# Seven products of two-by-two parts in place of eight, for the queries and values of a graph attention layer

## The chip, the core and the metric

The kernel runs on one core of a Trainium2 chip. The metric is the device time of one execution in microseconds (us), as the median of several runs. The engines named below are TensorE (PE in the profile; PEld are its weight loads), VectorE (DVE), ScalarE (ACT), and SyncE (SP), which issues the transfers. Each engine takes its instructions from a queue of its own, in order, and waits there until what an instruction needs is ready.

## The reference

Four graph layers stand one after the other, each as `x = x + layer(relu(layernorm(x)))`, on `x` of 128 graphs x 64 nodes x 256 features in float32. The first is a graph convolution, the second a spectral one (eigenvectors), the third a graph network with LSTMs over windows of nodes, and the fourth, where the change lies, an attention over the 512 edges of the graph with 4 heads of 64:

```python
Xq = (H @ W_lin.T).reshape(bt, n, h, dh)
Xv = (H @ W_val.T).reshape(bt, n, h, dh)
Qs, Kt = Xq[:, src], Xq[:, dst]
e = einsum('behd,hd->beh', leaky_relu(Qs + Kt, 0.2), a) + log(A0[src, dst] + eps)
attn = softmax of e over the edges of one source
Y = segment_sum(attn[..., None] * Xv[:, dst], src)
return Y @ W_out.T
```

The change concerns the first two lines: the queries `Xq` and the values `Xv`, two products of the same 8192 x 256 matrix with 256 x 256 weights.

## The kernel before

All matrices are float32. In the fourth layer (`layer3`) the 8192 rows are cut into 16 blocks of 512 rows (`BT`), a block into 4 tiles of 128 rows (`TPB`). Half a block, 256 rows or 4 graphs, is a group `g`; eight groups share one softmax (`q = g // 8`). Steps of the loop over `g`:

- `turned` normalizes a block (ACT writes `h`, one instruction a tile, from statistics `n_st`, `n_mv`, `n_r`, `n_m` of DVE) and transposes it on PE (`ps<-ident,h`) into `hT`: two chunks of 128 features, each 128 x 512. DVE copies the first chunk out of PSUM, ACT the second (`move` takes the two in turn).
- `queries` multiplies each of the 4 tiles with `WQV` (`w3_qv`, 256 x 512: columns 0 to 255 are `W_lin`, 256 to 511 are `W_val`) in two accumulating matmuls of 512 columns, one for each chunk. ACT copies the left half to `Q`, DVE the right half to `V` (tile `XV`). Then DVE multiplies `Q` with the vector `a` (`lin_p`) and sums it up by heads (`lin`).
- `score` is 8 matmuls (`ps<-ed_S,Q`), each followed by a ReLU on ACT (`r`). `reduce` is 8 matmuls of `r` into the bank `acc` (`acc<-r,ed_apad`). `softmax` works on DVE and ACT on a whole `acc` (tiles `sm_e`, `sm_m`), and `edgewise` transposes its result into `at`.
- `between` builds the attention matrices: DVE forms four products `aw` of 1024 columns for a group, PE sums them (`ps<-aw,ed_ODT`), ACT copies the sum to `an`. There are 5 buffers of `aw`, so DVE waits for PE to release one. `weighted` is 16 small matmuls of `an` with `V`, whose result DVE and ACT copy to `y` in halves. `output` is 4 matmuls (`ps<-w_o,y`) and an addition on DVE into `X`, which is then stored.
- `back`, in the first eight groups, transposes the third layer's result (`ls_t`) for a block and adds it to `X`.

`turned` and `queries` run one block ahead of `score`, in the odd groups. `between`, `weighted` and `output` run 10 groups behind it (`LAG`), so that blocks 6 and later have all the steps, and the earlier ones only a part. The pool `l3ps` has 5 PSUM banks for all tiles `ps`.

The order in which the steps are written is not quite the order in the queues: a scheduler in the framework sets, when the kernel is built, the order of each engine's instructions by its own estimate of durations, and the chip keeps to it. For an ordinary block the queue of PE before the change is: transposes, `output`, the eight matmuls of `queries`, `score`, `weighted`, `reduce`, `between`, then for the second half `output`, `score`, `weighted`, `reduce`, `between`.

Every operation is recorded under the line of a helper (L799), so groups are told apart by the names of their tiles.

Of the kernel before, what the change touches and what calls it, by code (L numbers as in the profile page):

```python
# [8 lines left out]
F32 = mybir.dt.float32  # L9
I32 = mybir.dt.int32  # L10
AF = mybir.ActivationFunctionType
# [64 lines left out]
class Eig:  # L76
# [12 lines left out]
    def t(self, name, *shape, dt=F32):  # L89
        key = (name, shape)  # L90
        if key not in self.tiles:
            n = "e_" + name + "_" + "_".join(map(str, shape))
            self.tiles[key] = self.pool.tile([64, *shape], dt, name=n)
        return self.tiles[key]
# [748 lines left out]
class Plan:  # L843
# [56 lines left out]
    def rest(self):  # L900

        while any(self.queue.values()):
            for e in self.queue:
                self.fill(e, 1e9)
# [8 lines left out]
class Fast:  # L913
# [229 lines left out]
    def scale(self):  # L1143
# [32 lines left out]

        Q = t("Q", 64, 2, 64)
        o.ts(Q[:, 0, :], D[:], mid[:], ALU.subtract, sc[:], ALU.mult)
        nes = self.NE = t("NEs", 64, 64)
        o.ts(nes[:], NE[:], sc[:], ALU.mult)  # L1180
        o.stt(Q[:, 1, :], nes[:], -1.0, nes[:], ALU.mult, ALU.mult)
        self.ne2 = Q[:, 1, :]
        p = self.mm((self.k.ones[0:1, :], Q[0:1, :, :].rearrange("p a b -> p (a b)")), p=128, n=128)
        DD, E2 = self.DD, self.E2 = t("DD", 128, 64), self.ME[:, 1, :]
# [258 lines left out]
B, N, D = 128, 64, 256  # L1443
P = 128
NB = 16
TPB = 4
BT = 512
# [18 lines left out]
class Kernel:  # L1466
# [949 lines left out]
    def layer3(self):  # L2416
        nc, o, io = self.nc, self.o, self.io
        cx, (w,) = self.stage([("l3x", 1)], "tile")
        with cx:
            cy, pools = self.stage([("l3", 2), ("l3v", 2), ("l3s", 1), ("l3r", 6), ("l3ps", 5), ("l3cps", 1), ("l3yps", 1)], "tile")  # L2420
            with cy:
                self.a02 = self.everywhere(w, "ed_a", io["L3_gnn_a"].rearrange("h d -> (h d)"))
                o.ts(self.a02[:], self.a02[:], 0.2, ALU.mult)
                self.drop, self.dropr = (w.tile([P, E], F32, name="ed_" + n) for n in ("drop", "dropr"))
                o.ts(self.drop[:], self.cont[:], 1.0, ALU.subtract, FLOOR, ALU.mult)
                o.ts(self.dropr[:], self.contr[:], 1.0, ALU.subtract, FLOOR, ALU.mult)
                WQV = w.tile([P, 2, 2 * D], F32, name="w3_qv")
                for x, n in enumerate(("W_lin", "W_val")):
                    nc.sync.dma_start(WQV[:, :, x * D:(x + 1) * D],
                                      io[f"L3_gnn_{n}_t"].rearrange("(k p) m -> p k m", p=P))  # L2430
                WO = self.weights(w, "w3_o", io["L3_gnn_W_out_t"])


                st, LAG = {}, 10
                self.turned(st, 0, *pools)
                self.queries(st, 0, WQV, *pools)
                for g in range(8 * NG + LAG + 2):
                    v, busy = g - LAG, g < 8 * NG
                    ahead = (g + 1) // 2 if g % 2 and g + 1 < 8 * NG else None
                    if busy:  # L2440
                        self.score(st, g, *pools)
                    if busy and v >= 1:
                        self.weighted(st, v - 1, *pools)
                    if busy:
                        self.reduce(st, g, *pools)
                    if g % 8 == 1 and 1 < g < 8 * NG + 2:
                        self.edgewise(st, g // 8 - 1, *pools)
                    if 0 <= v < 8 * NG:
                        self.between(st, v, *pools)
                    if not busy and v <= 8 * NG:  # L2450
                        self.weighted(st, v - 1, *pools)
                    if busy and g % 8 == 7:
                        self.softmax(st, g // 8, *pools)
                    if ahead:
                        self.turned(st, ahead, *pools)
                    if g < 8:
                        self.back(8 + g, pools[4], "ps")
                    if busy and v >= 1:
                        self.output(st, v - 1, WO, *pools)
                    if not busy and g > 8 * NG:  # L2460
                        self.output(st, v - 2, WO, *pools)
                    if ahead:
                        self.queries(st, ahead, WQV, *pools)

    def turned(self, st, i, pool, vp, sp, rp, psum, psc, psy):

# [2 lines left out]
        for dc in range(2):  # L2469
# [2 lines left out]
                self.nc.tensor.transpose(p[:, j * P:(j + 1) * P], h[:, j, dc * P:(dc + 1) * P], self.ident[:])  # L2472
            self.move(hT[:, dc, :], p[:])

    def queries(self, st, i, WQV, pool, vp, sp, rp, psum, psc, psy):

        o, hT = self.o, st["hT"]
        Q = rp.tile([P, TPB, D], F32, name="Q", bufs=2)
        V = st["V", i] = rp.tile([P, TPB, D], F32, name="XV", bufs=7)
        st["Q", i] = Q  # L2480
        for j in range(TPB):
            p = psum.tile([P, BT], F32, name="ps")
            for kc in range(2):
                self.mm(p[:], hT[:, kc, j * P:(j + 1) * P], WQV[:, kc, :], kc == 0, kc == 1)
            self.act(Q[:, j, :], p[:, 0:D], AF.Copy)
            o.copy(V[:, j, :], p[:, D:2 * D])

        if i % 4 == 0:
            st["lin", i // 4] = pool.tile([P, 2, 2, 8, HEADS], F32, name="lin")
            self.nc.vector.memset(st["lin", i // 4][:], 0.0)  # L2490
        lin, pr = st["lin", i // 4], sp.tile([P, TPB, D], F32, name="lin_p")
        o.mul(pr[:], Q[:], self.a02[:, None, :].to_broadcast([P, TPB, D]))
        k = 2 * (i % 4)
        for x in range(2):
            s = slice(64 * x, 64 * x + 64)
            o.red(lin[s, x, :, k:k + 2, :].rearrange("p m a h -> p a m h"),
                  pr[s].rearrange("p (a m) (h d) -> p a m h d", m=2, h=HEADS), ALU.add)
# [161 lines left out]
```

## Time and profile before

| | |
|---|---|
| median of 3 runs | 2345.04 us (2342.6 to 2351.49) |
| profiled execution | 2348.6 us, of it the span of the profile 2346.8 us |
| mean granted clock of TensorE | 0.993 |
| PE busy | 2293.6 us |
| DVE busy | 1602.6 us |
| ACT busy | 1134.3 us |
| fourth layer | from about 1750 us to the end |
| 1900 to 2250 us of the span | PE 349.38, DVE 201.44, ACT 138.67 of 350 us busy |

A line of a group gives line, engine, operation, output<-inputs, partitions x elements and the number of records, then the busy time in us, the mean of one in ns, and the idle time of the engine ahead of it with what ended it. A float32 matmul leaves two records, so that 256 records are 128 matmuls. A line of the timeline gives the start and the duration in us, the engine, and in brackets the idle time ahead of it and its releaser. A matmul's recorded end is modelled and reaches over the start of the next one, so the time that PE needs for a row of matmuls is read from start to start.

### The profile page before, as it was taken

The numbers are of one execution on the slowest core, as the hardware profiler recorded it, in microseconds if no ns is written. First come the engines' busy times: TensorE is split into PE (matmuls) and PEld (weight loads), VectorE is DVE, ScalarE is ACT, GpSimd is POOL, SyncE is SP. The second block draws the span as 40 slices with busy tenths as digits, with TensorE's granted clock in tenths as the row PEclk, the third lists the DMA queues.
The fourth block names the chain that finished last, engine by engine and source line by source line (L and its number), as shares of the span: only waits on it lengthen the run. The fifth ranks groups of instructions, "written<-read, shape, count | busy, mean of one in ns | idle before, by whom it ended". The sixth has DMA issues, their size and how long they took to land.

```text
span 2346.8 us, 32591 instructions
## 1 busy us (share of the span) xinstructions
PE 2293.6 (98%) x12153; PEld 1629.2 (69%) x12153; DVE 1602.6 (68%) x4006; ACT 1134.3 (48%) x2490; POOL 2.9 (0%) x26
## 2 busy tenths in 40 slices
PE   7999998999999999999999999999999999999989
PEld 4555446986777788888999998888874444444434
DVE  7877676998447777666777667569655566556467
ACT  5665864654436654444444434347445544344321
POOL 0000000000000000000000000000000000000000
PEclk9999999999999999999999999999999999999989
DMA  5000221230010000001000001000020000000001
GB/s 170 1 2 19 64 63 27 73 82 19 1 36 1 1 19 1 1 1 37 1 1 1 1 14 59 1 1 17 1 72 1 1 10 14 14 19 14 15 14 50
DMA packets 61192, 54.86 MB, mean 23 GB/s; under 512 B 15203, under 2 KB 58852, under 8 KB 61028
## 3 DMA queue, kind: packets, MB, share of 16 engines
q1 hardware_dynamic: 61028, 52.73, 7.3%
q8 instruction: 96, 1.57, 0.3%
q14 instruction: 68, 0.56, 0.1%
HBM read 35.93 MB, written 16.78 MB: 22 GB/s over the span
## 4 chain that ended last, share of the span: by engine, by line
PE 80%; DVE 3%; issue 0%; ACT 0%; ACTq 0%; DVEq 0%
PE ps L799 69%; PE acc L799 5%; PE pt L799 4%; PE pe L799 1%; DVE sm_m L799 1%; PE y L799 1%; DVE X L799 1%; DVE aw L799 0%; ACT ls_g L799 0%; DVE ls_g L799 0%; DVE sm_e L799 0%; DVE ls_t L799 0%; DVE XV L799 0%; DVE y L799 0%; DVE n_st L799 0%
## 5 line engine op out<-in xcount | busy, mean ns | idle before, releaser
L799 ACT ACTIVATE ls_g<-ls_g,ls_b 128x512 f32<-128x512 f32 (+4 forms) x472 | 242.9, 565 | 153.2 <-DVE ls_g L799 151.4
L799 ACT ACTIVATE ls_g<-ps,ls_b 128x256 f32<-128x256 f32 (+3 forms) x268 | 115.3, 470 | 330.6 <-PE ps L799 327.3
L799 PE MATMUL ps<-z,w 128*128 128x512 f32 x512 | 259.1, 630 | 0.9 <-ACT z L799 0.9
L799 PE MATMUL ps<-big,X 128*128 128x176 f32 (+3 forms) x848 | 212.9, 366 | 0.8 <-ACT big L799 0.7
L799 DVE TENSOR_TENSOR aw<-at,ed_OST 128x1024 f32<-128x1024 f32 x128 | 150.0, 1220 | 92.7 <-PE ps L799 92.7
L799 DVE TENSOR_TENSOR ls_g<-ls_z,ps 128x512 f32<-128x512 f32 (+5 forms) x256 | 146.9, 579 | 91.4 <-PE ps L799 90.0
L799 PE MATMUL ps<-ls_tx,X 128*128 128x160 f32 (+2 forms) x960 | 207.0, 326 | 0.6 <-ACT ls_g L799 0.6
L799 PE MATMUL ps<-X,X 128*128 128x160 f32 (+1 forms) x896 | 199.1, 306 | 0.0
L799 PE MATMUL ps<-X,ls_w 128*128 128x256 f32 x640 | 190.5, 379 | 0.0
L799 PEld LDWEIGHTS ps<-ls_tx,X 128*128 128x128 f32 x960 | 161.8, 190 | 15.4 <-DVE X L799 5.2
L799 PEld LDWEIGHTS ps<-big,X 128*128 128x128 f32 x848 | 145.9, 190 | 30.6 <-issue 19.4
L799 DVE TENSOR_TENSOR X<-ls_g 128x1024 f32<-128x1024 f32 (+2 forms) x108 | 117.4, 1087 | 51.1 <-ACT ls_g L799 51.1
L799 ACT ACTIVATE r<-ps 128x512 f32<-128x512 f32 x256 | 129.3, 625 | 41.4 <-PE ps L799 41.3
L799 PEld LDWEIGHTS ps<-X,X 128*128 128x128 f32 x896 | 148.4, 190 | 0.0
L799 PE MATMUL ps<-X,ls_s 128*128 128x256 f32 x480 | 142.3, 379 | 0.0
L799 PEld LDWEIGHTS ps<-z,w 128*128 128x128 f32 x512 | 88.8, 193 | 71.1 <-issue 62.6
L799 PE MATMUL ps<-ls_tx,ls_s 128*128 128x256 f32 x464 | 134.7, 379 | 0.0
L799 PE MATMUL ps<-ls_tx,ls_w 128*128 128x256 f32 x464 | 133.3, 380 | 0.0
L799 PEld LDWEIGHTS ps<-X,ls_w 128*128 128x128 f32 x640 | 121.4, 190 | 16.8 <-DVE X L799 0.3
L799 PE MATMUL ps<-big,ls_w 128*128 128x256 f32 x464 | 131.9, 379 | 0.7 <-ACT ls_z L799 0.7
L799 PE MATMUL ps<-ed_S,Q 64*128 64x512 f32 x512 | 128.3, 617 | 0.9 <-DVE XV L799 0.9
L799 ACT ACTIVATE h<-X,n_m,n_r 128x256 f32<-128x256 f32 x192 | 99.6, 589 | 40.9 <-issue 25.0
(532 smaller groups left out, 4012.0 us busy)
## 6 DMA issues: line engine op xcount, KB each, us to landing
X<-in_x_dram SPq DMA_DIRECT2D x32, 512.0 KB
xs<-X SPq DMA_DIRECT2D x16, 512.0 KB
X<-xs SPq DMA_DIRECT2D x16, 512.0 KB
out_dram<-X SPq DMA_DIRECT2D x32, 256.0 KB
X<-in_L_gnn_Wih_t_dram SPq DMA_DIRECT2D x4, 512.0 KB
ls_w<-in_L_gnn_Wih_t_dram SPq DMA_DIRECT2D x4, 512.0 KB
ls_w<-in_L_gnn_Whh_t_dram SPq DMA_DIRECT2D x4, 512.0 KB
w<-in_L_gnn_W_t_dram SPq DMA_DIRECT2D x2, 512.0 KB
```

The costliest lines, as they stand in the source:

```text
L799: i = method(*a, **kw)
```

## The change

The queries and values of a block are seen as one product of two-by-two parts. `A[t][k]` is `hT`'s chunk `k` (128 features) of the 256 rows `t`; `B[k][x]` is chunk `k` of `W_lin` (`x = 0`) or `W_val` (`x = 1`). The 4 results, queries and values of the two halves of the rows, took 8 products of parts. They now take 7, by Strassen's scheme in Winograd's form; a product of parts is two matmuls of 256 columns, one for each tile of 128 rows, so that a block has 14 matmuls of 256 columns instead of 8 of 512.

`sums3` forms four sums of the weights once, on DVE. In a block DVE forms three sums of `hT` ahead of the products (S3, S1 in the place of `A[1][0]`, S2) and a fourth later; all are 128 x 256. Product 1 goes to PSUM bank a, 6 to b, 7 to f, 5 to d; ACT copies bank a to `Z` (half of `V`), and only then does product 2 add into bank a, which ACT copies to half of `Q`. DVE adds b to `Z`, forms `U` (the other half of `V`) from `Z` and f, and adds d to `U`; after that products 4 and 3 add into f and d, and two further additions on DVE give the other half of `Q` and finish `Z`. `queries` now returns its second part (`rest`: products 2, 4 and 3 and their results), which is called after `output`, the first part being called ahead of it. `Q` has one buffer instead of two. The work on `lin` is the same, in a function of its own.

In the built kernel the queue of PE for an ordinary block is now: transposes, `weighted`, products 1, 2, 6, 7, 5, `output`, products 4 and 3, `score`, `reduce`, `between`; its second half is as before. In blocks 9 and 13 six of the sixteen matmuls of `weighted` stand between products 1 and 2.

```diff
--- before.py
+++ after.py
@@ -2433,7 +2433,8 @@
 
                 st, LAG = {}, 10
                 self.turned(st, 0, *pools)
-                self.queries(st, 0, WQV, *pools)
+                WQV = self.sums3(w, WQV)
+                self.queries(st, 0, WQV, *pools)()
                 for g in range(8 * NG + LAG + 2):
                     v, busy = g - LAG, g < 8 * NG
                     ahead = (g + 1) // 2 if g % 2 and g + 1 < 8 * NG else None
@@ -2455,12 +2456,14 @@
                         self.turned(st, ahead, *pools)
                     if g < 8:
                         self.back(8 + g, pools[4], "ps")
+                    if ahead:
+                        rest = self.queries(st, ahead, WQV, *pools)
                     if busy and v >= 1:
                         self.output(st, v - 1, WO, *pools)
                     if not busy and g > 8 * NG:
                         self.output(st, v - 2, WO, *pools)
                     if ahead:
-                        self.queries(st, ahead, WQV, *pools)
+                        rest()
 
     def turned(self, st, i, pool, vp, sp, rp, psum, psc, psy):
 
@@ -2472,18 +2475,59 @@
                 self.nc.tensor.transpose(p[:, j * P:(j + 1) * P], h[:, j, dc * P:(dc + 1) * P], self.ident[:])
             self.move(hT[:, dc, :], p[:])
 
+    def sums3(self, w, WQV):
+
+        o = self.o
+        B = [[WQV[:, k, D * x:D * x + D] for x in range(2)] for k in range(2)]
+        T1, T2, T3 = (w.tile([P, D], F32, name=f"w3_t{n}")[:] for n in range(3))
+        o.sub(T1, B[1][1], B[0][1])
+        o.sub(B[0][1], B[0][1], B[0][0])
+        o.sub(T2, B[1][1], B[0][1])
+        o.sub(T3, B[1][0], T2)
+        return {1: B[0][0], 2: B[1][0], 3: B[1][1], 5: B[0][1], 7: T1, 6: T2, 4: T3}
+
     def queries(self, st, i, WQV, pool, vp, sp, rp, psum, psc, psy):
 
         o, hT = self.o, st["hT"]
-        Q = rp.tile([P, TPB, D], F32, name="Q", bufs=2)
+        A = [[hT[:, k, 256 * t:256 * t + 256] for k in range(2)] for t in range(2)]
+        S = sp.tile([P, 2, 256], F32, name="hS")
+        S1, S2, S3 = A[1][0], S[:, 0], S[:, 1]
+        o.sub(S3, A[0][0], A[1][0])
+        o.add(S1, A[1][0], A[1][1])
+        o.sub(S2, S1, A[0][0])
+        Q = st["Q", i] = rp.tile([P, TPB, D], F32, name="Q", bufs=1)
         V = st["V", i] = rp.tile([P, TPB, D], F32, name="XV", bufs=7)
-        st["Q", i] = Q
-        for j in range(TPB):
-            p = psum.tile([P, BT], F32, name="ps")
-            for kc in range(2):
-                self.mm(p[:], hT[:, kc, j * P:(j + 1) * P], WQV[:, kc, :], kc == 0, kc == 1)
-            self.act(Q[:, j, :], p[:, 0:D], AF.Copy)
-            o.copy(V[:, j, :], p[:, D:2 * D])
+        banks = {}
+
+        def product(a, m, bank, first):
+            if first:
+                banks[bank] = psum.tile([P, 2, D], F32, name="ps")
+            for u in range(2):
+                self.nc.tensor.matmul(banks[bank][:, u, :], a[:, u * P:(u + 1) * P], WQV[m], start=first and u == 0,
+                                      stop=u == 1, skip_group_check=True)
+            return banks[bank][:]
+
+        Z, U = V[:, 0:2, :], V[:, 2:4, :]
+        a = product(A[0][0], 1, "a", True)
+        self.act_copy(Z, a)
+        o.add(Z, Z, product(S2, 6, "b", True))
+        o.add(U, Z, product(S3, 7, "f", True))
+
+        o.sub(S3, A[0][1], S2)
+        o.add(U, U, product(S1, 5, "d", True))
+
+        def rest():
+            self.act_copy(Q[:, 0:2, :], product(A[0][1], 2, "a", False))
+            o.add(Q[:, 2:4, :], Z, product(A[1][1], 4, "f", False))
+            o.add(Z, Z, product(S3, 3, "d", False))
+            self.linear(st, i, pool, vp, sp, rp, psum, psc, psy)
+
+        return rest
+
+    def linear(self, st, i, pool, vp, sp, rp, psum, psc, psy):
+
+        o, Q = self.o, st["Q", i]
 
         if i % 4 == 0:
             st["lin", i // 4] = pool.tile([P, 2, 2, 8, HEADS], F32, name="lin")
```

## The prediction

> **What bounds the kernel now.** I read the page's busy shares first, then the waits of TensorE (PE) in the fourth layer, then the groups by form for durations, then the timeline of one block. Last I read the order of the instructions in the engines' queues, before and after the change, which is fixed when a kernel is built.
>
> Page, parts 1 and 2; after it all waits of PE between 1900 and 2250 us (us in total, times, longest):
> ```profile
> PE 2293.6 (98%) x12153; PEld 1629.2 (69%) x12153; DVE 1602.6 (68%) x4006; ACT 1134.3 (48%) x2490; POOL 2.9 (0%) x26
> PE   7999998999999999999999999999999999999989
> PE ps L799 <- DVE XV L799: 0.6, 1, 0.6
> ```
> PE never rests in this layer: 0.6 us in 350. So PE time saved is saved in full, and every new wait of PE is paid in full.
>
> Groups (busy us, mean ns of one); then two rows from the timeline of the third layer's Strassen products:
> ```profile
> L799 PE MATMUL ps<-w_qv,hT 128*128 128x512 f32 x256 | 112.7, 593 | 0.7 <-DVE hT L799 0.7
> L799 DVE TENSOR_TENSOR ls_tx<-big,ls_tx 128x256 f32<-128x256 f32 x96 | 40.3, 420 | 1.1
> L799 DVE TENSOR_TENSOR X<-X,ps 128x512 f32<-128x512 f32 x48 | 32.1, 681 | 19.4 <-PE ps L799 19.2
> 1500.21 0.59 PE L799 MATMUL ps<-ls_tx,ls_w 128*128 128x256 f32 x2
> 1500.64 0.59 PE L799 MATMUL ps<-X,ls_w 128*128 128x256 f32 x2
> ```
> A 256-column matmul comes every 0.43 us (1500.64 - 1500.21). An addition on VectorE (DVE) takes 0.42 for 256 columns, 0.68 for 512 out of PSUM.
>
> Timeline of one block (start, duration):
> ```profile
> 2049.22 3.50 DVE L799 TENSOR_TENSOR aw<-at,ed_OST 128x1024 f32<-128x1024 f32 x3 [4.84 <-PE ps L799]
> 2050.84 1.09 PE L799 MATMUL ps<-ident,h 128*128 128x128 f32 x8
> ...
> 2051.77 1.89 PE L799 MATMUL ps<-w_o,y 128*128 128x256 f32 x8
> 2051.97 0.60 ACT L799 ACTIVATE hT<-ps 128x512 f32<-128x512 f32 x1 [0.39 <-PE ps L799]
> 2052.46 2.06 ACT L799 ACTIVATE h<-X,n_m,n_r 128x256 f32<-128x256 f32 x4
> 2052.63 0.68 DVE L799 COPY hT<-ps 128x512 f32<-128x512 f32 x1
> ...
> 2053.50 7.03 PE L799 MATMUL ps<-w_qv,hT 128*128 128x512 f32 x16
> ...
> 2055.41 0.38 ACT L799 ACTIVATE Q<-ps 128x256 f32<-128x256 f32 x1 [0.89 <-PE ps L799]
> ...
> 2060.46 3.91 PE L799 MATMUL ps<-ed_S,Q 64*128 64x512 f32 x16
> ...
> 2064.92 3.65 PE L799 MATMUL acc<-r,ed_apad 128*64 128x512 f32 x16
> ```
> What the reader is to see: the transposes of `turned` end at 2051.77, but the DVE copy of hT ends only at 2053.31, since three `aw` products stand before it. The output projection (`w_o`, 1.73 us) fills exactly that hole.
>
> **What the change saves.** The 8 matmuls take 2060.46 - 2053.50 = 6.96 us; 14 of 0.43 take 6.03. That is 0.93 a block, and over 16 blocks 15 us. ScalarE (ACT) does two copies of 0.60 for four of 0.38, 0.3 less. DVE does four additions of 0.42 and five of 0.68 for four copies of 0.42: 3.4 more a block. It is busy 201 of 350 us here, so on average it has room; what counts is where these stand in its queue.
>
> **What the change costs: an ordinary block** (6, 7, 9 to 11, 13 to 15). PE's queue is now: transposes, the 16 small `weighted` matmuls (0.62, before behind the scores), product 1, 2, 6, 7, 5, `output`, 4, 3, scores. On the clock above:
> - The transposes and `weighted` end at 2052.39. Product 1 needs hT: 2053.31 + 0.05 = 2053.36. `output` no longer covers: 0.97 idle.
> - Product 1 ends at 2054.22. Product 2 adds into its bank, so ACT must first have copied it to V. In ACT's queue hT and four h stand before (to 2054.52), a half of y (0.40) and the copy (0.60, as for hT): 2055.52, product 2 at 2055.57. Idle 1.35. With ACT free it would still be 0.20 (from the end of two matmuls, 2055.21, to the Q copy at 2055.41) + 0.60 + 0.05 = 0.85.
> - Product 6 needs the sum S2. DVE after hT: y 0.42, S3 0.42, one `aw` 1.22, S1 0.42, a reciprocal 0.17, S2 0.42: 2056.38. Product 2 ends at 2056.43; no wait, with nothing to spare.
> - Products 6, 7, 5 end at 2059.02, `output` at 2060.75. DVE has read product 7's bank by about 2060.0 and product 5's by 2061.1, so products 4 and 3 run on, to 2062.47. Here `output` is the cover; without it 0.6 to 1.0 more.
> - Scores: the sixth needs the bank of product 3, which DVE reads only after the residual, Q and lin_p: 2065.1 against 2064.6. The eight take 3.98 instead of 3.84. `acc` starts at 2066.45, in the trace at 2064.92: **+1.5**.
>
> Eight such blocks: +12.
>
> **Blocks with a softmax, 8 and 12.** There the softmax is mixed with the new sums in DVE's queue. From the timeline of block 8:
> ```profile
> 1980.38 1.22 DVE L799 TENSOR_TENSOR_SCAN sm_m<-ed_drop,sm_e 128x512 f32<-128x512 f32 x1
> ...
> 1991.32 3.34 DVE L799 RECIPROCAL sm_m<-sm_m 128x512 f32<-128x512 f32 x1
> 1991.46 1.98 PE L799 MATMUL ps<-ed_S,Q 64*128 64x512 f32 x6 [0.62 <-DVE XV L799]
> ```
> Before S2 come two scans (2.2), S3, a maximum, S1 and a subtraction: S2 at 1985.2, product 2 ends at 1983.5, idle 1.7. Before product 5 is read come y, `aw`, two additions, two scans, a product and S3: 1992.4, where PE would be ready for product 3 at 1990.8. Before Q comes the reciprocal of 3.34: Q at 1997.8 frees the last score's bank. `acc` starts at about 1998.2 instead of 1995.05: +3.1 each, +6.
>
> **Early blocks**, by the same reckoning on their own timelines:
> - Blocks 1 to 3 have no `output` or `weighted` yet, and ACT's `ls_t` copy of 1.13 and two h stand before V's copy: product 2 idles 1.7, less 0.93, +0.7 each, +2.
> - Block 0: two DVE operations of 1.22 stand among the sums. hT ends at 1751.1, S2 at 1754.9, product 1 at 1752.7: idle 2.2, and 0.7 before product 4; less 0.93, +2.
> - Block 4 (softmax, no `aw`): hT ends at 1851.4; two scans, two residual additions, a maximum, a subtraction and the sums put S2 at 1857.7, product 2 ends at 1854.5: idle 3.2. Products 4 and 3 wait 1.1 and 1.0 behind scans and reciprocal. Less 0.93: +4.3.
> - Block 5: three `aw` among the sums put S2 at 1883.0, product 2 ends at 1881.2: 1.8. V's copy costs 1.1, the last score's bank 1. Less 0.93: +3.
>
> Together +11.
>
> **Beside the path.** The four weight sums are 1.7 us of DVE, once, in the third layer's end, where PE waits 1.5 us in 150: priced 0, between -1 (order changes) and +1.7. Q's single buffer: its last reader, the scores of the block before, ends some 10 us earlier: 0. Behind the last block nothing changes.
>
> Sum: 12 + 6 + 11 = **+29.6** unrounded. The profiled execution took 2348.6 (span 2346.8 and 1.8 around it), 3.6 above the median; it would become 2378. On the median: 2345 + 30 = **2375**. Bounds: only the 0.97 and the least copy wait of 0.85 in eight ordinary blocks (+0.9 each) and half of all the rest give +16; a third more on everything gives +39.
>
> **The clock.** Two idle times of PE near the end:
> ```profile
> 2270.71 0.69 PE L799 MATMUL y<-an,XV 64*64 64x64 f32 x32 [2.71 <-ACT y L799]
> ...
> 2279.68 1.12 PE L799 MATMUL ps<-ident,sm_e 128*128 128x128 f32 x4 [8.27 <-DVE sm_e L799]
> 2280.72 5.90 PE L799 MATMUL ps<-aw,ed_ODT 128*64 128x512 f32 x16
> ```
> Up to the end of 2.71 us idle the granted clock is 0.98 (2262 to 2272); during the 8.27 it falls to 0.50, and the two groups after it take 2.7 us longer than elsewhere (5.90 for 3.65, 1.12 for 0.66). My longest gap, 3.2 us, is nearest to the first: 0. Three such falls at the top of the range: +8.
>
> [...]
>
> **Rivals.**
> - The holes are covered, and PE keeps its saving: 2345 - 15 = 2330, faster. It decides between products 1 and 2 and before product 1: the two gaps must come to less than 0.93 a block. For it: in blocks 9 and 13 six `weighted` matmuls stand between products 1 and 2. Against it: in the others nothing does, and PE's queue is in order. 3%.
> - Only the copy of V shows, at its least (0.85), with DVE early enough everywhere: -0.93 + 0.85 = -0.1 a block, and up to +0.5 with ACT's queue: 2343 to 2353, no change. The `aw` that stand before hT in both kernels speak against it. 9%.
> - The gaps reach the length that halves the clock, in most of 16 blocks at 2.7: 2375 + 30 or more, 2405. Only the 8.27 us row speaks for it. 6%.
> - The products do not become shorter: the two rows at 0.43 exclude it, as weights and columns have the same shape.
>
> **Numbers.** The forecast has 82%. Range 2360 to 2393: from +16, to +39 with three falls of the clock (+47). A change of 0.5% (11.7 us) is about what a measurement of this kernel can tell from none. Faster 3%, same 9%, slower 88% (82 + 6).
>
> **What would show it.** Right: PE busy falls by about 15 us in the layer while its waits rise from 2.4 us (1750 to 2250) to some 45, most before product 1 (on hT), before product 2 (on XV by ACT), and in blocks 4, 5, 8 and 12 on hS or XV by DVE. Wrong: waits under 15 us in all; the wait on hT missing, as DVE's `aw` came earlier; a granted clock under 0.9 between 1750 and 2250.

## The result and the profile after

The changed kernel takes **2375.61 us** (median of four runs, 2373.75 to 2380.73) against 2348.2 of the kernel before on the same chip: the ratio is 1.0124, with a 95% interval of 1.0107 to 1.014. It is slower by 27.4 us, where 30 more than 2345 had been forecast.

The comparison of the two traces needs one caution. The span grew by 26.0 us only (2346.8 to 2372.8), because the first 400 us, which the change does not touch, ran 4 us shorter in this execution. So everything below goes by the length of the fourth layer alone, from the first transposes of block 0 to the end of the span: 597.1 us before, **627.5 after, +30.4**. A block's length is read from its transposes to those of the next. All these lengths are of one profiled execution of each kernel; where nothing differs, the blocks of two kernels agree within 0.01 us.

The page's busy shares, then TensorE's (PE's) waits from 1750 to 2250 us (us in total, times, longest):

```profile
PE 2292.5 (97%) x12345; PEld 1662.1 (70%) x12345; DVE 1651.1 (70%) x4090; ACT 1124.9 (47%) x2455; POOL 2.9 (0%) x26
```
```profile
PE ps L799 <- ACT XV L799: 11.7, 13, 1.4
PE ps L799 <- DVE hS L799: 5.6, 5, 1.6
PE ps L799 <- DVE hT L799: 4.8, 6, 0.8
PE ps L799 <- DVE n_r L799: 3.3, 2, 2.7
...
```

Where PE waited 2.4 us in these 500, it now waits 27.5 (two rows of 1.5 and 0.6 are left out), most of it on V's copy by ACT, on hT and on the sums hS (the row `n_r` is a wait ahead of product 6 too). VectorE (DVE) is busy 48.5 us more and still rests 30% of the span.

The timeline of block 10, the block that the prediction reckoned on (start, duration, then idle time and releaser):

```profile
2067.92 0.69 PE L799 MATMUL y<-an,XV 64*64 64x64 f32 x32
...
2068.69 0.69 DVE L799 COPY hT<-ps 128x512 f32<-128x512 f32 x1
...
2069.43 1.13 PE L799 MATMUL ps<-w_qv,hT 128*128 128x256 f32 x4 [0.82 <-DVE hT L799]
...
2070.75 0.58 ACT L799 ACTIVATE XV<-ps 128x512 f32<-128x512 f32 x1
...
2071.38 1.13 PE L799 MATMUL ps<-w_qv,hT 128*128 128x256 f32 x4 [0.82 <-ACT XV L799]
...
2071.54 0.42 DVE L799 TENSOR_TENSOR hS<-hT 128x256 f32<-128x256 f32 x1
...
2072.35 1.89 PE L799 MATMUL ps<-w_t,hS 128*128 128x256 f32 x8
...
2074.94 1.89 PE L799 MATMUL ps<-w_o,y 128*128 128x256 f32 x8
...
2076.67 1.03 PE L799 MATMUL ps<-w_t,hT 128*128 128x256 f32 x4
...
2077.53 1.03 PE L799 MATMUL ps<-w_qv,hS 128*128 128x256 f32 x4
...
2078.49 3.91 PE L799 MATMUL ps<-ed_S,Q 64*128 64x512 f32 x16
```

Every step of the reckoned block can be seen. The transposes (from 2066.90) and `weighted` are done at 2068.54, hT at 2069.38, product 1 starts at 2069.43: 0.89 idle. Product 1 ends at 2070.30 (0.87 after its start), V's copy at 2071.33, product 2 starts at 2071.38: 1.09 idle. S2 is there at 2071.96, before product 2 ends: no wait. `output` stands between products 5 and 4, and neither product 4 nor 3 waits; the scores start at 2078.49. The block is 1.34 us longer than before.

### The profile page after: what moved, and what is told of

It is laid out like the page before. It is cut to its first block, busy times and chain, and to the rows that moved or that the text cites. A ratio compares the mean times of both kernels' runs of the same rounds, so it can differ in the third digit from the quotient of the medians.

```text
span 2372.8 us, 33131 instructions
## 1 busy us (share of the span) xinstructions
PE 2292.5 (97%) x12345; PEld 1662.1 (70%) x12345; DVE 1651.1 (70%) x4090; ACT 1124.9 (47%) x2455; POOL 2.9 (0%) x26
## 4 chain that ended last, share of the span: by engine, by line
PE 78%; DVE 4%; ACT 1%; issue 1%; SPq 0%; DMA 0%; ACTq 0%; DVEq 0%
PE ps L799 68%; PE acc L799 5%; PE pt L799 4%; DVE sm_m L799 1%; PE pe L799 1%; DVE aw L799 1%; PE y L799 1%; DVE X L799 0%; ACT h L799 0%; ACT ls_g L799 0%; DVE hT L799 0%; DVE sm_e L799 0%; DVE hS L799 0%; ACT XV L799 0%; DVE ls_g L799 0%
## 5 line engine op out<-in xcount | busy, mean ns | idle before, releaser
L799 PE MATMUL ps<-ed_S,Q 64*128 64x512 f32 x512 | 134.0, 619 | 1.5 <-ACT r L799 1.5
```

Of the source, the lines that this page charges most:

```text
L799: i = method(*a, **kw)
```

## Experiments

Each run's whole time, and the length of the fourth layer, which is what the theories are about (the last column is the layer's). The first three kernels, the fifth and the ninth were executed four times or more, the others once:

| kernel | us | fourth layer | against before |
|---|---|---|---|
| before | 2348.2 | 597.1 | |
| after | 2375.6 | 627.5 | +30.4 |
| transposes and sums early | 2350.1 | 600.2 | +3.1 |
| before, transposes early | 2356.3 | 605.4 | +8.3 |
| early, h behind the relus | 2339.8 | 591.0 | -6.1 |
| before, early, h behind the relus | 2346.4 | 593.0 | -4.1 |
| before, nine DVE operations more | 2355.0 | 604.4 | +7.3 |
| after, softmax behind the products | 2375.6 | 621.7 | +24.6 |
| early, h behind, softmax of 8 and 12 late | 2348.7 | 597.7 | +0.6 |
| after, scores behind product 3 | 2384.1 | 631.2 | +34.1 |
| after, output ahead of the products | 2381.8 | 628.6 | +31.5 |
| after, product 2 behind 5 | 2397.4 | 644.5 | +47.4 |
| the same with three idle matmuls | 2379.7 | 634.1 | +37.0 |
| after, order 1, 7, 2, 6, 5 | 2373.3 | 620.7 | +23.6 |

**Is it the order or the work?** The first pair moves the transposes and the sums half a block ahead, with and without the seven products:

```diff
-                    if ahead:
-                        self.turned(st, ahead, *pools)
...
+                    if g % 2 == 0 and g + 2 < 8 * NG:
+                        self.turned(st, g // 2 + 1, *pools)
+                        self.hsums(st, g // 2 + 1, *pools)    # S3, S1, S2; only with the seven products
```

With the products:

> The changed kernel, but the transposes of a block (with the copies into hT) and its three sums S3, S1 and S2 are put half a block earlier in the order, at the end of the group before, so that hT and S2 are done long before product 1. Measure: the fourth layer's length, from the first transposes of block 0 to the end of the span (597.1 us before the change, 627.5 after it). My theory: the loss is idle time of TensorE on hT, on V's copy and on S2, made by where these stand in the queues, and not the additional work of VectorE; with hT and the sums early, ACT has h behind it when V's copy comes, and TensorE keeps most of the 15 us: the layer takes 584 to 594, 3 to 13 less than before the change, the whole 2331 to 2342. Waits of TensorE on hT and hS go, from 11 us to under 3. Rival (the 3.4 us of VectorE a block are the price, wherever they stand): the layer stays at 617 or more, the waits only take another name (DVE XV, DVE Q).

Without them:

> The kernel before the change, with nothing but the transposes of a block put half a block earlier. It separates what the earlier transposes bring by themselves from what the products bring. My theory: TensorE has no waits there to lose, so the layer takes 597 within 2 us, and any gain of the kernel with early transposes and seven products is owed to the products. Rival (the earlier order is by itself better, products or not): 592 or less.

The ratio of the first to the kernel before is 1.0015 (1.0003 to 1.0027): 27 of the 30 us are gone with the same work on every engine, so the rival (VectorE's load is the price) falls. But the layer took 600.2, not 584 to 594, although the waits on hT and hS were down to 2.6. And the second run was 8.3 longer than the kernel before, where 2 at most was expected, with no wait of PE in the layer's list at all. Its timeline shows why:

```profile
2044.79 4.94 PE L799 MATMUL ps<-ed_S,Q 64*128 64x512 f32 x16
...
2046.51 0.59 ACT L799 ACTIVATE h<-X,n_m,n_r 128x256 f32<-128x256 f32 x1
...
2047.00 0.58 ACT L799 ACTIVATE r<-ps 128x512 f32<-128x512 f32 x1
2047.47 0.59 ACT L799 ACTIVATE h<-X,n_m,n_r 128x256 f32<-128x256 f32 x1
2047.63 0.29 PEld L799 LDWEIGHTS ps<-ed_S,Q 64*128 64x128 f32 x2 [0.68 <-ACT r L799]
2047.97 0.59 ACT L799 ACTIVATE r<-ps 128x512 f32<-128x512 f32 x1
```

The eight scores behind the early transposes take 4.87 us (2044.79 to 2049.66) instead of 3.84. In ACT's queue h and the relu r go in turn, so that a score's bank comes free only every 0.97 us. The row of PE names no wait, since the modelled ends of its matmuls cover it; the row of its weight loads (PEld) does.

**The saving, found.** So h was put behind the last relu of the odd group, an order on ACT alone:

```diff
-                        self.turned(st, g // 2 + 1, *pools)
+                        self.turned(st, g // 2 + 1, *pools, after=st.get(("relu", g - 1)))
...
+            x = self.nc.scalar.activation(h[:, j, :], ...)
+            if after is not None:
+                self.behind(x, after)      # a place in ACT's queue, no wait
```

> The kernel with the transposes and sums half a block early, and with the four activations that make h put behind the last relu of the odd group's scores in ACT's queue (an order on one engine, no new work). In the run with early transposes alone TensorE has no named wait in an ordinary block, but its row of eight scores behind the transposes takes 4.87 us instead of 3.84, because ACT's queue runs h and relu in turn and frees a score's bank only every 0.97 us. My theory: this row is the place where the products' saving went; behind the change it takes 3.9 again, an ordinary block falls by 0.9 to 1.0, and the fourth layer's length falls from 600.2 us to 583 to 590 (597.1 before the change), the whole to 2331 to 2338. Rival (the row is slow for another reason, such as the transposes ahead of it): the row keeps 4.8 or more and the layer 598 or more.

> The kernel before the change with the transposes half a block early and h behind the relus: the same order without the seven products. My theory: the row of scores takes 3.9 again and the layer 596 to 599, as before the change, so that what the seven products bring is the difference to the same order with them, 0.8 to 0.9 us a block, 9 to 14 in all. Rival (the order itself is the gain): 590 or less.

With the seven products, from the timeline of PE:

```profile
2040.60 3.97 PE L799 MATMUL ps<-ed_S,Q 64*128 64x512 f32 x16
2044.50 0.69 PE L799 MATMUL y<-an,XV 64*64 64x64 f32 x32
...
2052.14 1.13 PE L799 MATMUL ps<-w_qv,hT 128*128 128x256 f32 x4
2053.11 1.89 PE L799 MATMUL ps<-w_t,hS 128*128 128x256 f32 x8
2054.83 1.03 PE L799 MATMUL ps<-w_qv,hT 128*128 128x256 f32 x4
2055.70 1.89 PE L799 MATMUL ps<-w_o,y 128*128 128x256 f32 x8
2057.42 1.03 PE L799 MATMUL ps<-w_qv,hT 128*128 128x256 f32 x4
2058.29 1.03 PE L799 MATMUL ps<-w_t,hT 128*128 128x256 f32 x4
2059.15 1.03 PE L799 MATMUL ps<-w_qv,hS 128*128 128x256 f32 x4
2060.11 3.91 PE L799 MATMUL ps<-ed_S,Q 64*128 64x512 f32 x16
```

The row of scores behind the transposes takes 3.90 again (2040.60 to 2044.50), and no product waits: the fourteen matmuls take 6.25 us (2052.14 to 2060.11, less 1.72 for `output`). An ordinary block is 33.79 long against 34.61 in the same order with eight products: **0.82 saved**, as the mechanism says. This version beats both kernels: 2339.77 us, ratio to before 0.997 (0.9957 to 0.9984). Its layer of 591.0 missed the expected 583 to 590 by a little, and against the same order without the products (593.0, itself under the 596 to 599 expected) only 2 us are left of 9 to 14. The rest goes back in the blocks that are not ordinary: +1.44 in block 0, where product 6 waits on S2; +1.85 in block 4, where the granted clock falls to 0.50 for 3.41 us (1.7 us of work); +0.55 in block 5; +1.36 and +1.15 in blocks 8 and 12, where product 4 waits 0.88 and 0.53 on VectorE, in whose queue the softmax stands.

**VectorE's load alone.** Work that nobody uses, behind the copies of the queries, in the kernel before:

```diff
+        for k in range(4):
+            o.sub(S[:, k % 2], hT[:, k % 2, 0:256], hT[:, k % 2, 256:512])
+        for k in range(5):
+            o.add(pr[:, 0:2, :], V[:, 0:2, :], V[:, 2:4, :])
```

> The kernel before the change with nine additional VectorE operations a block, behind the copies of the queries (four of 256 columns on hT and five of 512 on V, whose results nobody uses), and Q in one buffer; TensorE's work and its order stay. It takes VectorE's additional load alone: 5.1 us of work a block, 81 in all, more than the change adds. My theory: VectorE is busy 201 of 350 us there and TensorE does not wait for it, so the layer grows by 0 to 8 us. Rival (VectorE's load is the price): 20 to 30 more, with waits of TensorE on DVE.

The layer grew by 7.3, at the upper end of the theory. The eleven blocks 1 to 3, 6, 7, 9 to 11 and 13 to 15 start their `acc` at the same time after their transposes as before, within 0.01 us. The loss is in the blocks with a softmax: +6.0 in block 4 (where 6.83 us at half clock are 3.4 of it), +1.2 in 8, +2.1 in 12; block 5 and the tail give 1.9 back. VectorE's load has no price in an ordinary block; it has one where the softmax fills the queue.

**The softmax.** In the changed kernel its call was moved behind `rest()`:

```diff
-                    if busy and g % 8 == 7:
-                        self.softmax(st, g // 8, *pools)
...
                     if ahead:
                         rest()
+                    if busy and g % 8 == 7:
+                        self.softmax(st, g // 8, *pools)
```

> The changed kernel with the softmax of a group of four blocks put behind the products instead of ahead of the transposes. By the prediction blocks 4, 8 and 12 lose 4.3, 3.1 and 3.1 us because the softmax stands among the sums in VectorE's queue; measured were 3.5, 2.4 and 4.0. My theory: without it they lose what their neighbours lose, 1.3 to 1.9 each, so the layer is 4 to 7 us shorter than after the change, 621 to 624; the other blocks stay within 0.3 each. Rival (the late sums there come from the weighted products, which stay): 627 within 1.5.

The layer takes 621.7, within 621 to 624, but not as expected in every block. A matmul of the softmax moves from one block to the next, so pairs are compared: blocks 7 and 8 lose 1.5 instead of 3.7, blocks 11 and 12 lose 1.9 instead of 5.4, and blocks 3 and 4 lose 7.0 instead of 5.4. For 8 and 12 the theory stands. In block 4 the late softmax makes a later row of scores wait 2.9 us (ACT r), and the granted clock falls there for 6.83 us.

The same in the best order, for blocks 8 and 12 (the softmax of block 4 also moves, but only behind the first part of the products):

> The kernel with early transposes and sums and h behind the relus (fourth layer 591.0 us, against 593.0 for the same order with the eight products), and with the softmax of blocks 8 and 12 put behind the products in the order (that of block 4 stays ahead of the output projection). In that order the seven products save 0.82 an ordinary block, but give 1.36 and 1.15 back in blocks 8 and 12, 1.85 in block 4 and 1.44 in block 0. My theory: in 8 and 12 it is the softmax between the additions in VectorE's queue, as in the changed kernel, where putting it behind took 2.2 and 3.4 off the pairs 7 and 8 and 11 and 12: here it takes 1.5 to 2.5 off each pair, the layer takes 586 to 588.5 and the whole is 0.4 to 0.6% under the kernel before the change. Rival (what is late there is the residual and Q, which stay): the layer stays at 590 to 592, the whole at 0.3%.

A miss: 597.7, ratio to before 1.0007 (0.9996 to 1.0018). Blocks 8 and 12 did fall by 0.7 and 1.0, but PE waits 5.0 us on DVE's X in the blocks behind them. In block 9 the residual X, which frees a bank for the third score, comes only behind the softmax's reciprocal (3.35 us, to 1999.02), one more operation of it and three `aw`, at 2003.08 to 2003.76. Moved behind, the softmax makes the next block wait: blocks 9 and 13 rise by 2.7 and 4.1 (13 with a fall of the clock of 3.41 us).

**Blocks 1 to 3.** There a score stands alone between products 5 and 4:

```profile
1779.72 1.12 PE L799 MATMUL ps<-ed_S,Q 64*128 64x512 f32 x2
1780.77 1.13 PE L799 MATMUL ps<-w_t,hT 128*128 128x256 f32 x4
1781.74 1.03 PE L799 MATMUL ps<-w_qv,hS 128*128 128x256 f32 x4
1782.69 3.70 PE L799 MATMUL ps<-ed_S,Q 64*128 64x512 f32 x14
```

Alone it takes 1.05 us (1779.72 to 1780.77), the seven others 3.63, all eight in one row 3.84. The scores were held behind product 3:

```diff
+                m = self.nc.tensor.matmul(p[:], Q[...], self.S2[s, :], start=True, stop=True)
+                if g % 2 == 0:
+                    self.behind(m, st["P3"])      # product 3's last matmul
```

> The changed kernel with the scores of an even group held behind product 3 on TensorE. In blocks 1 to 3 one score stands between products 5 and 4 and takes 1.05 us there, the seven others 3.63; in a row the eight take 3.84, since two scores on the two halves of the rows run side by side. The prediction did not have this and took 0.7 a block for blocks 1 to 3, where 1.88 was measured. My theory: the lone score is the difference, blocks 1 to 3 fall by 0.7 to 0.9 each; the ordinary blocks have it too and fall by less than that, 0 to 0.8; the layer 627.5 becomes 614 to 625. Rival (the score stood in a hole that product 4 would have had anyway): the blocks 1 to 3 stay within 0.2 and a wait before product 4 of 0.8 or more comes up.

Blocks 1 to 3 fell by 0.78 each, as expected. The ordinary blocks did not change (their scores stood behind product 3 anyway; the expectation was wrong that they have a lone score). Block 4 rose by 5.0, and there the rival holds: its scores had filled a hole, and product 3 now waits 4.1 us on DVE (two falls of the clock by 3.41 us each come on top). So the layer rose to 631.2 instead of falling to 614 to 625.

**The cover.** The output projection went ahead of all products:

```diff
-                    if ahead:
-                        rest = self.queries(st, ahead, WQV, *pools)
                     if busy and v >= 1:
                         self.output(st, v - 1, WO, *pools)
...
                     if ahead:
-                        rest()
+                        self.queries(st, ahead, WQV, *pools)()
```

> The changed kernel with the output projection ahead of all seven products, as before the change. By the prediction's steps the wait on hT goes in an ordinary block (0.89 us there), V's copy still makes product 2 wait at least 0.85, and products 4 and 3 lose their cover and wait 0.6 to 1.0 more on VectorE's reads of their banks. My theory: the two cancel, an ordinary block changes by -0.5 to +0.5, the layer takes 620 to 633; the wait on hT is gone from TensorE's list and one on DVE XV has come. Rival (the output projection would have covered the loss, so that its place is the fault): an ordinary block falls by 1 or more, the layer to 615 or less.

The layer takes 628.6, and an ordinary block changes by -0.14 to +0.12 (block 14 by +0.26): they cancel. The wait on hT is gone from 5.6 to 0.7, that on V's copy from 12.4 to 6.9 (between 1740 and 2300 us). What came instead is no named wait: `weighted` is broken up into three pieces, and without the cover a lone score of 1.05 us again stands between two products. The output projection fills one hole, not two. (Blocks 4, 8 and 12 rise by 0.9 to 1.0 each, and in each of them the clock now falls for 3.41 us, while the fall in block 5 is gone.)

**V's copy.** Product 2 was held behind product 5:

```diff
+                if m == 2 and u == 0:
+                    self.behind(x, done[5])
```

> The changed kernel with product 2 held behind product 5 on TensorE, so that V's copy by ACT has 2.6 us more to land. It undoes the wait on V's copy alone (12.4 us on TensorE's list, 1.09 in an ordinary block by the starts). My theory: a wait removed alone brings up the next: product 6 then stands behind product 1 and waits for S2, which VectorE ends 1.66 us after product 1's end in block 10; an ordinary block changes by +0.3 to +0.8, blocks 1 to 3 by -0.4 to +0.4, the layer takes 627 to 635; TensorE's list shows hS where it showed ACT XV. Rival (V's copy is a price by itself): an ordinary block falls by 0.8 or more and the layer to 617 or less.

The wait changed its name as expected (ACT XV gone, hS 26.4 us), but the layer took 644.5, far over 627 to 635. In the timeline of PE, and in the busy time of the stretches (length, then PE, PEld, DVE, ACT and POOL, then the granted clock):

```profile
2083.18 1.13 PE L799 MATMUL ps<-w_qv,hT 128*128 128x256 f32 x4 [0.82 <-DVE hT L799]
2085.77 3.67 PE L799 MATMUL ps<-w_t,hS 128*128 128x256 f32 x8 [1.46 <-DVE hS L799]
```
```profile
2083.00:2085.70 2.70, 1.13 (x4) 0.68 (x4) 2.70 (x8) 2.08 (x5) 0.00 (x0) 1.00 0.03 6
2085.80:2089.20 3.40, 3.40 (x8) 2.77 (x9) 1.19 (x4) 0.00 (x0) 0.00 (x0) 0.50 0.00 0
```

Products 6 and 7 take 3.50 us (product 5 starts at 2089.27) instead of 1.73, at a granted clock of 0.50, and no idle time before them is longer than 1.46. Nine stretches of the layer before 2250 us, 3.41 us each, run at half clock (one in the changed kernel). Blocks 6, 11 and 14 have none, and there the expectation holds: +0.64, +0.64 and +0.78. In 7, 9, 10 and 13, with one each, it is +2.3 to +2.55. Three matmuls with no use were put into the hole to test that:

```diff
+        for u in range(3):
+            self.nc.tensor.matmul(banks["b"][:, u % 2, :], A[0][0][:, 0:P], WQV[1], start=u != 1, stop=True, ...)
```

> The kernel with product 2 behind product 5 (fourth layer 644.5 us, 17 more than the changed kernel, where 0 to 8 more were expected), with three matmuls more in every block between products 1 and 6, of 256 columns and with a result that product 6 writes over. In the run without them the granted clock falls to 0.50 for 3.41 us in nine places of the layer; in block 10 products 6 and 7 take 3.50 us there instead of 1.73, behind two idle times of TensorE of only 0.82 and 1.46 us. My theory: the clock falls where TensorE has been idle for some 2 us of a stretch of 3.41, in one piece or in several, so work that nobody needs, put into the hole of 1.72 us before product 6, keeps it up: at most two falls are left, products 6 and 7 take 1.73 again, and the layer takes 627 to 634, less than without the added work. Rival (the slow products come from something else, the banks or hS): the three matmuls only add, up to 1.3 a block, and the layer takes 644 to 665.

The layer is **10.4 us shorter with more work**: 634.1, at the edge of the theory. Two falls are left (blocks 4 and 5), and in block 10 products 6 and 7 take 1.83. Blocks 7, 9, 10 and 13 became 1.67 to 1.92 shorter, while 6, 11 and 14, which had no fall to lose, kept their length within 0.01: the three matmuls cost nothing in the hole, and what they bring is the clock:

```profile
2073.05 1.99 PE L799 MATMUL ps<-w_t,hS 128*128 128x256 f32 x8 [0.17 <-DVE hS L799]
2074.88 1.03 PE L799 MATMUL ps<-w_qv,hT 128*128 128x256 f32 x4
```

Last, the hole was filled with product 7, which needs only S3:

```diff
-        o.add(Z, Z, product(S2, 6, "b", True))
-        o.add(U, Z, product(S3, 7, "f", True))
+        f = product(S3, 7, "f", True)
+        self.act_copy(Q[:, 0:2, :], product(A[0][1], 2, "a", False))
+        o.add(Z, Z, product(S2, 6, "b", True))
+        o.add(U, Z, f)
```

> The changed kernel with the products in the order 1, 7, 2, 6, 5: product 7 needs only S3, which VectorE makes first, and fills TensorE's wait for V's copy by ACT with work of its own. It takes the wait on V's copy away without bringing the one on S2 in its place. My theory: in block 10 product 1 ends at 2070.30, product 7 at 2071.17, V's copy lands at 2071.33, so product 2 waits 0.2 instead of 1.09 and everything behind it comes 0.9 earlier; the same in most blocks, 14 of them, so the layer takes 612 to 619 (627.5 for the changed kernel, 597.1 before the change): V's copy was a third to a half of the loss, and the wait on hT and the rest stay. Rival (behind the copy something else is as late, S2 or the banks): the layer stays at 623 or more.

620.7 lies between the two: a miss. An ordinary block falls by 0.86 and blocks 1 to 3 by 0.85, as expected; blocks 0, 4 and 8 rise by 0.7, 1.1 and 1.6, 4 and 8 with a fall of the clock that the changed kernel did not have there. The wait on V's copy is worth 0.84 to 0.87 in each of ten blocks (up to their `acc`), and 6.8 us net.

## Why the prediction was right, point by point

The mechanism was right: the products are shorter, and the new waits on hT, on V's copy and on S2 cost more than they save. That the total fits so well (+30.4 in the layer for +29.6) is in part luck: the ordinary blocks were put 2 us too high and blocks 1 to 3 3.6 too low. That the whole time of 2375.6 meets 2375 to the microsecond is luck as well, since the kernel before took 2348.2 beside it, 3 more than the forecast started from.

- **The saving** was put at 0.93 a block (14 matmuls at 0.43). It is 0.82 where nothing waits (the pair with h behind the relus). The fourteen take 6.25 instead of 6.03, because at two places it is 0.96 to 0.97 to the next start instead of 0.87: 2052.14 to 2053.11 and 2059.15 to 2060.11 above. In both, the weights of a matmul (product 1's first, the first score) are loaded only as it starts, and not 0.21 us before it as elsewhere; for products and output projection this run's trace has 32 such records, and each takes 0.28 to 0.38 to the next one instead of 0.22.
- **An ordinary block** was put at +1.5 and took +1.34 to +1.42 in six of the eight, and +1.2 in blocks 14 and 15 up to their `acc`. The wait on hT was 0.89 (forecast 0.97), that on V's copy 1.09 (1.35: ACT's operations start 0.49 apart, closer than their durations of 0.6), product 6 had none, products 4 and 3 had none behind `output`. In blocks 9 and 13 it came about otherwise: no wait on hT, which `weighted` covers, but 0.59 (by PE's list) before product 6. The slower starts (0.96 to 0.97 for 0.87, as above) took 0.22 of an ordinary block. The sixth score's bank did not cost the 0.14 that the sum had for it. Eight blocks: +10.0 for +12 (block 15 with the tail behind it, +0.6).
- **Softmax blocks 8 and 12**: +2.4 and +4.0 for +3.1 each, +6.4 for +6. That the softmax in DVE's queue is the cause is shown by putting it behind. The steps differ from the reckoned ones, though: by the starts S2 costs 1.28 instead of 1.7, and a lone score stands between products 4 and 3 here too.
- **Blocks 1 to 3** are the mis-sized term: +1.88 each against +0.7. The lone score is 0.78 of it, shown by moving it. The rest is argued from the starts: four products at 0.95 to 0.97 where 0.87 was taken, 0.4.
- **Blocks 0, 4 and 5**: +1.5, +3.5 and +3.4 for +2, +4.3 and +3. In block 4 the waits of 1.1 and 1.0 reckoned before products 4 and 3 shrank to one of 0.60, since six of the eight scores stand ahead of product 3. In block 5 the sum was right for a wrong reason, by the next point.
- **The clock** was put at nothing, by the longest single gap. This failed in block 5:

```profile
1886.39 1.13 PE L799 MATMUL ps<-w_qv,hT 128*128 128x256 f32 x4 [0.80 <-ACT XV L799]
1888.86 3.65 PE L799 MATMUL ps<-w_t,hS 128*128 128x256 f32 x8 [1.34 <-DVE hS L799]
```
```profile
1885.40:1888.80 3.40, 1.32 (x5) 0.68 (x4) 3.40 (x7) 2.03 (x4) 0.00 (x0) 1.00 0.00 0
1888.80:1892.20 3.40, 3.34 (x8) 2.71 (x9) 2.30 (x4) 0.00 (x0) 0.00 (x0) 0.51 0.00 0
```

  Two gaps, 0.80 and 1.34 by PE's list, left PE busy for 1.32 of 3.40 us; the next 3.41 us ran at half clock, and products 6 and 7 took 3.49 instead of 1.73. That is 1.8 of the 30.4 us, and without it block 5 would have lost 1.7 instead of 3. A gap of 2.68 us in block 4, longer but alone, had no such effect here; the same gap of 2.68 in the run with the scores behind product 3 did have it. Counted in steps of 3.41 us from the falls, it lay whole within one stretch there, and in block 4 only 1.97 of it did (1858.12 to 1860.09). That this makes the difference was not tested. The row that the prediction went by was misread, too: in the kernel before, the half clock begins at 2271.63, only 0.2 us into the 8.27 us, at the end of a stretch of 3.41 us that holds nearly all of the gap of 2.71 (PE busy for 0.69 us of it, granted clock 1.00). So that row spoke for a fall behind a gap of 2.7 us, not against it. The range had three falls in it.
- **What would show it.** The named waits were to be some 45 us and are 27.5. The sum counted from start to start, and the list counts from modelled ends, which hide 0.1 to 0.3 of every wait and the lone scores altogether. For the same reason the products' busy time in the groups did not fall: 112.7 us before, 51.9 + 32.5 + 17.1 + 16.7 = 118.2 after. The sum of the steps was right, this check of it was not.
- **The rivals.** Covered holes (2330) were reached in part only, and in another order than the change has: early transposes with h behind the relus take 2339.8, and most of that gain is the order's own (-4.1 of -6.1 us in the layer). "Only the copy of V shows" is excluded by the run that fills that wait: 23.6 us are left. The clock halved in most blocks (2405) did not come: one fall. The products do become shorter, by 0.82 a block. VectorE's load by itself was rightly put at nothing for ordinary blocks.

## What to carry to other kernels

Fewer instructions on the engine that bounds a kernel are worth something only if the new dependencies fit into its queue: here seven products for eight saved 0.82 us a block and the first order cost 2.2, because each sum and copy sat behind work of the same engine that could have waited. Look for independent work to stand between a producer and its consumer, in the order of the queue, before trusting the count; and ask of every move what it is put in front of on the other engines (early transposes pulled h in among the relus and cost 1.0 a block without any named wait). When PE's row shows no wait and still runs slow, read the row of its weight loads and compare starts.

## What the hardware showed that was not expected

- The half clock does not need one long gap. In block 5 of the changed kernel it came behind a stretch of 3.41 us with gaps of 0.80 and 1.34 (PE busy for 1.32 of 3.40 us), in block 10 of the run with product 2 behind 5 behind gaps of 0.82 and 1.46, and in the kernel before, at 2271.63, behind one gap of 2.71. In the traces before and after it lasts 3.41, 6.83 or 13.65 us at a time, and in the changed kernel the half clock at 2298.44 begins 409.60 us behind that of block 5 at 1888.84, 120 times 3.413. Counted back from there in steps of 3.413, one stretch with 1.97 idle (block 4 of the changed kernel) had no fall behind it. At a granted clock of 0.50 a fall cost 1.7 us of PE's work for each 3.41. In block 4 of the best version it came behind less idle time than any of these: a gap of 1.07 us, ahead of which stands a matmul of a single row of 1.1 us (`ed_log,ones`); products 4 and 3 then take 3.50 us (1860.81 to 1864.31) instead of 1.82. No run shows why.
- Two scores on the two halves of the rows run side by side: in the trace of the kernel before their matmuls start 7 ns apart, and the pair takes 0.96 us (2060.46 to 2061.42). One alone takes 1.05 (1779.72 to 1780.77 in the changed kernel), so a scheduler that uses a single score as filler pays for two.
